# A graph layer's steps: the PSUM copies on VectorE, four more columns a step on ScalarE, another order at the beginning

## The chip, the cores and the metric

The kernel runs on one core of one Trainium2 chip. The metric is the device time of one execution in microseconds (us). A profile of one execution shows TensorE (PE for matmuls, PEld for the loading of weights), VectorE (DVE), ScalarE (ACT), GpSimd (POOL), SyncE (SP) and the DMA queues; a "q" behind an engine's name (ACTq, DVEq, SPq) marks instructions that its sequencer alone works off, such as register loads and DMA issues. PSUM is the memory that TensorE writes to, SBUF the working memory.

## The reference: what is computed

A message-passing layer on a graph of 12,500 nodes (64 features each) and 212,500 edges (32 features each), sorted by destination, with a residual and a layer norm:

```python
msg_in = concat([nodes[row], nodes[col], edge_features])      # 64 + 64 + 32
messages = relu(msg_in @ mW1 + mb1) @ mW2 + mb2               # hidden 128, out 64
aggregated = segment_sum(messages, col, num_segments=12500)
upd_in = concat([nodes, aggregated])
new = relu(upd_in @ uW1 + ub1) @ uW2 + ub2
out = layernorm(x + new)
```

`row` is the source and `col` the destination of an edge.

## The kernel before

**Groups and steps.** The edges are cut into G = 554 groups of 384 (three tiles of 128). One pass of the loop at line 854 is one step k. TensorE's work in step k (`step`, line 806) belongs to three groups: `turn` (460) transposes the gathered source features and a one-hot of the destination of group k into PSUM (line 466, three transposes); `hidden` (487) multiplies the columns of group k-3 with the weights (492); `sums` (517) adds the ReLU results of group k-6 by destination with the one-hot (521). Two PSUM slots alternate (`SLOTS`), so that TensorE's step k waits until what step k-2 left in its slot has been read: by the copy of line 479 and by the ReLU of line 503. After TensorE's step k one instruction copies the transposes together with the sums (513 columns) from PSUM to the operand ring in SBUF (line 479, on ScalarE), and VectorE applies the ReLU for group k-3 (line 503). The last ten groups (`SHORT`) run in another, shorter order.

**Three ways to a group's source features.** Most come by GpSimd's indirect DMA, one for each tile of 128 edges (line 194), issued `AHEAD` = 16 groups ahead into a ring of `RING` = 20. For some groups, the `COPIED` ones, they aren't gathered: the whole transposed node table lies in SBUF (`own.xc`), and ScalarE and VectorE copy single columns of it into the operand ring. The column's address is loaded into a register first (`registers`, 689, the loads are at line 702), then `fetch` (709) issues the copies: VectorE two columns with one instruction (line 725), ScalarE one column with each (line 728). In a step VectorE makes columns in portions of `VCOLS` = (12, 8, 8), ScalarE in portions of `ACOLS` = (8, 4, 4, 4, 4); each portion is one load of that many registers and then its copies. That is 52 columns a step from step 18 on (`BEGIN`), which makes 71 groups `COPIED`. They are complete one step before the group's `turn` step, three before the `hidden` step that reads them. For eight tiles SP fetches single rows (line 783).

**VectorE's order in a step** is ReLU, load of 12 registers, 6 pairs, the one-hot of a later group (line 440), load of 8, 4 pairs, load of 8, 4 pairs. **ScalarE's** is copy, load of 8, 8 columns, then four times load of 4, 4 columns. Every 8 steps VectorE turns the next node numbers into addresses (lines 681 and 687).

**Beginning.** In the first 25 steps `projected(k)` (402) makes the destination half of the first product for 512 nodes: TensorE (407), a ScalarE copy to one of three scratch buffers `t` (410) and a DMA to the table `by_dst` (411). In the first 16 steps `bit(k)` (252) loads a further part of the node table and of the source numbers. `window(g)` (414) loads 32 rows of `by_dst` for group g (line 430); it is issued in step g-4, behind everything that has been stored to `by_dst` so far (`written`). All these DMAs go through SP's queue in program order. At step 8 (`CHECKED`) the sortedness of the edges is checked.

**Updates.** When a chunk of nodes has all its sums (`PLAN`, line 75; 512 nodes, the last full chunk in two halves of 256), `update` (538) works it off in twelve stages, one for each step: its partial sums are loaded (560) and joined on TensorE (571), VectorE moves them out of PSUM (598), three products follow on TensorE (576, 615, 616), a ReLU on ScalarE (621), the last products (627, 628) and the layer norm. All use the one PSUM buffer `u_ps`.

Of the kernel before, what the change touches and what calls it, by code (L numbers as in the profile page):

```python
# [10 lines left out]
F32 = mybir.dt.float32  # L11
# [3 lines left out]
AF = mybir.ActivationFunctionType  # L15
# [5 lines left out]
P = 128  # L21
N = 12500
# [10 lines left out]
G = (E + GE - 1) // GE  # L33
SB = 4
AHEAD = 16
RING = AHEAD + 4
BLOCKS = 4
NW = 8
SLOTS = 2
# [5 lines left out]
AT = BANK - GE  # L45
# [3 lines left out]
CH = 512  # L49
NEAR_NODES = 1024  # L50
NEAR_GROUPS = 16
BITS = 16
LIMITS = (0, 12, 18)
SHORT = 10
# [4 lines left out]
VCOLS = (12, 8, 8)  # L59
ACOLS = (8, 4, 4, 4, 4)  # L60
PAIRED = sum(VCOLS)
# [13 lines left out]
def plan():  # L75


    import math

    def least(g):  # L80
        q = min(1.0, g * GE / E)
        return g * GE * N / E - 6.0 * math.sqrt((E - N) * q * (1 - q)) * N / E - 6

    chunks, b = [], 0
    whole = N // CH * CH
    for e in [*range(CH, whole, CH), whole - CH // 2, whole, N]:
        chunks.append((b, e - b, next((g for g in range(G) if least(g) >= e), G)))
        b = e
    return chunks
# [46 lines left out]
def ordered(ctx: ExitStack, tc: tile.TileContext, a, own, ok):  # L136
# [3 lines left out]
    nc = tc.nc  # L140
    x, out = a["x"], a["out"]
    const = ctx.enter_context(tc.tile_pool(name="const", bufs=1))
    dram = ctx.enter_context(tc.tile_pool(name="dram", bufs=1, space=DRAM))
    rowp = ctx.enter_context(tc.tile_pool(name="rows", bufs=3))
    iop = ctx.enter_context(tc.tile_pool(name="iota_ps", bufs=1, space=PSUM))
# [3 lines left out]
    temp = early.enter_context(tc.tile_pool(name="temp", bufs=1))  # L149
    ident, wm = own.ident, own.wm  # L150
    xc = own.xc[:, 1 : 2 * NP + 1].rearrange("p (n s) -> p n s", s=2)[:, :, 0]
    xc_bytes = own.xc.bitcast(U8)
# [11 lines left out]
    efs_by, hidden_by, marks_by = {}, {}, {}  # L164
# [111 lines left out]
    halves = [(0, G // 2), (G // 2, G)]  # L276
    firsts_f = [own.pre[k][:, : g1 - g0] for k, (g0, g1) in enumerate(halves)]
    for f, (g0, g1) in zip(firsts_f, halves):
# [15 lines left out]

    high = temp.tile([1, G], F32, name="high")
    nc.vector.memset(high, float(N - 1))
    for g0, g1 in zip(LIMITS, [*LIMITS[1:], FIRST_FREE]):
        nc.vector.memset(high[:, g0:g1], float(CH * (1 + max(1, g0 - 6)) - W))
    start_f = temp.tile([1, G], F32, name="start_f")
    start_b = const.tile([1, G, 2], I32, name="start_b")  # L300
# [37 lines left out]
    store_by = {}  # L338
    written = []

# [10 lines left out]
    def ordered_edges():  # L351
# [4 lines left out]
        nc.vector.tensor_scalar(off, dlc, W - 1.0, 0.0, ALU.is_le, ALU.add, accum_out=valid[:, 1:2])  # L356
        low = temp.tile([1, G], F32, name="low")
        opens = [0, *(closes for *_, closes in PLAN)]
# [4 lines left out]
        nc.vector.memset(high[:, 0:1], 0.0)  # L363
        wrong = temp.tile([1, 2, G], F32, name="wrong")
        nwrong = temp.tile([1, 2], F32, name="nwrong")
        first_f = start_f
        nc.vector.tensor_copy(first_f, first_i[0:1, :])
        nc.vector.tensor_tensor(wrong[:, 0], first_f, low, ALU.is_lt)
# [33 lines left out]
    def projected(c):  # L402

        base, n = TABLE[c]
        ps = ups.tile([H, CH], F32, name="u_ps").rearrange("p (n h) -> p n h", n=4)
        for j in range(n):
            nc.tensor.matmul(ps[:, j], xc[: D + 1, base + j * P :][:, :P], w1b,  # L407
                             start=True, stop=True)
        t = rowp.tile([P, 4, H], F32, name="t")
        nc.scalar.activation(t[:, :n], ps[:, :n], AF.Copy)  # L410
        written.append(after(nc.sync.dma_start(
            by_dst[base : base + n * P, :].rearrange("(n p) h -> p n h", n=n), t[:, :n])))

    def window(g):
# [3 lines left out]
        if g % SB == 0:  # L418
# [6 lines left out]
            for i in range(n):  # L425
# [7 lines left out]
                "(w b) -> w b", w=W))  # L433
        after(wm_by[g], *written, *([hidden_by[g - NW]] if g >= NW else []))
        written.clear()

# [23 lines left out]
    def turn(g, ps):  # L460
# [11 lines left out]
        def copy(step):  # L472
            t, c, n = columns(g)
            turn_by[g] = step
            r = slice(D if g in columned else 0, D + W)
            if step in with_sums:
                n = GE + ROW
            copies = [ordered_by_steps(
                after(nc.scalar.activation(t[r, c : c + n], ps[r, AT : AT + n], AF.Copy), step))]  # L479
            if g >= BLOCKS * SB:  # L480
                after(copies[0], hidden_by[g - BLOCKS * SB])
            copy_by[g] = copies
            return copies
# [319 lines left out]
    ahead_of = {turn: 0, hidden: TO_HIDDEN, sums: TO_SUMS}  # L803
    with_sums, unstored = set(), []

    def step(*work):
# [17 lines left out]
        for part, g, _, _, follow in parts:  # L824
            users[part][(g + ahead_of[part]) % SLOTS] = follow(did[-1])
        unstored.extend(g for part, g in work if part is sums)
# [14 lines left out]
    for g in range(SB):  # L841
        window(g)
    nc.sync.dma_start(dlc_i[:, near:], a["dst_cols"][:, near:])
    update_weights()
    weights(NW)
    inputs(1)
    relative(NEAR_GROUPS, G)
    indexes(0)
# [5 lines left out]
    for k in range(G):  # L854
        if k < BITS:
            bit(k)
        if 1 < k < len(TABLE):
            projected(k)
        if k == CHECKED:
            addresses(0)  # L860
            for n in range(len(STREAMS)):
# [24 lines left out]
        if k < G - 1:  # L886
            registers(k, len(VCOLS))
        fetch(0)
        window(k + SB)
        stored()  # L890
# [370 lines left out]
```

## Time and profile before

| | us |
|---|---|
| median of 3 runs | 1848.74 (1846.92 to 1851.61) |
| the profiled execution | 1847.94 |
| its span in the profile | 1846.2 |
| ACT / DVE / POOL / PE busy in the span | 1602.8 / 1151.3 / 1362.1 / 1402.9 |
| mean granted TensorE clock | 0.939 |

The span is the time from the first to the last instruction that the profile shows; the execution is 1.7 us longer. A row of a group of instructions gives line, engine, operation, output<-input and shapes, the count, then busy time, the mean duration of one in ns, and the idle time of the engine just before them with what ended it. "issue" means that nothing which the profile shows was waited for. Loads of registers are not counted as busy time of an engine; the view of one line lists them with their shortest, median and longest duration. In the timeline a row starts with start and length in us.

### The profile page before, as it was taken

Reading aid. Unit: us, or ns where it says so; the run is one execution under the profiler, and the core shown is the slowest. Engines: PE = TensorE matmul, PEld = TensorE weight load, DVE = VectorE, ACT = ScalarE, POOL = GpSimd, SP = SyncE. Lnnn points to the kernel's source line nnn. Section 1 sums busy time; section 2 is a strip of 40 time slices with the busy share of each in tenths; the row PEclk is TensorE's granted clock in tenths of the full one; section 3 lists DMA queues with packets and bytes.
Section 4 is the critical chain, followed back from the end, with each engine's and each line's share of the span. In section 5 each row is a group of like instructions: output and inputs, shape, how many; then the busy total and the mean of one; then the engine's idle time right before and its main releaser. Section 6 shows DMA issues by size and latency. Waiting matters only on the chain. (4 is left out here: it accounts for less than half of the span.)

```text
span 1846.2 us, 57017 instructions
## 1 busy us (share of the span) xinstructions
PE 1402.9 (76%) x9841; PEld 1112.0 (60%) x9841; DVE 1151.3 (62%) x9034; ACT 1602.8 (87%) x13268; POOL 1362.1 (74%) x1447
## 2 busy tenths in 40 slices
PE   3677677877878878768778778777778778788677
PEld 3565565666656656556566566656656556566565
DVE  2315566666666666666666666666666666666652
ACT  2338799999999999899999999989999989989962
POOL 7777577777777777777777777777777777777772
PEclk9759899999999999999999999999989999999999
DMA  6653333333333333333333333333323333333331
GB/s 148 137 132 90 69 74 65 69 76 65 69 75 66 73 72 64 72 61 74 74 65 70 75 64 69 74 64 68 78 63 67 76 63 69 76 63 70 75 65 39
DMA packets 197393, 137.63 MB, mean 75 GB/s; under 512 B 62855, under 2 KB 172653, under 8 KB 196957
## 3 DMA queue, kind: packets, MB, share of 16 engines
q1 hardware_dynamic: 150166, 85.91, 18.7%
q0 software_dynamic: 46080, 47.25, 15.5%
q14 instruction: 288, 2.35, 0.4%
q8 instruction: 85, 1.39, 0.3%
q10 hardware_dynamic: 774, 0.72, 0.2%
HBM read 105.70 MB, written 28.00 MB: 72 GB/s over the span
## 5 line engine op out<-in xcount | busy, mean ns | idle before, releaser
L194 POOL DMA_INDIRECT own_rows<-in_x,src_sb x1440 | 1361.3, 945 | 451.0 <-issue 191.1
L728 ACT ACTIVATE own_operands<-own_xc 64x1 f32 x12576 | 1288.7, 189 | 16.5 <-issue 5.0
L725 DVE TENSOR_TENSOR own_operands<-own_xc 64x2 f32 x7344 | 666.9, 149 | 499.7 <-issue 496.3
L466 PE MATMUL own_ps<-own_ident,own_rows 128*96 128x128 f32 x1653 | 297.8, 292 | 329.9 <-ACT own_operands L728 208.6
L521 PE MATMUL own_ps<-own_h,own_rows 128*32 128x129 f32 x3322 | 491.3, 285 | 4.1 <-ACT own_operands L479 1.9
L492 PE MATMUL own_pre<-own_wm,own_operands 128*128 128x128 f32 x3322 | 490.2, 287 | 0.0
L466 PEld LDWEIGHTS own_ps<-own_ident,own_rows 128*96 128x96 f32 x1653 | 173.0, 133 | 460.4 <-ACT own_operands L728 273.1
L492 PEld LDWEIGHTS own_pre<-own_wm,own_operands 128*128 128x128 f32 x3322 | 443.8, 203 | 2.3 <-issue 1.4
L479 ACT ACTIVATE own_operands<-own_ps 96x513 f32<-96x513 f32 (+2 forms) x554 | 321.1, 580 | 96.0 <-PE own_ps L521 68.5
L503 DVE TENSOR_SCALAR own_h<-own_pre 128x384 f32<-128x384 f32 x553 | 300.4, 543 | 148.2 <-PE own_ps L521 106.9
L521 PEld LDWEIGHTS own_ps<-own_h,own_rows 128*32 128x32 f32 x3322 | 330.5, 113 | 82.7 <-issue 8.6
L440 DVE TENSOR_TENSOR own_rows<-iota,dlc 128x96 f32<-128x96 f32 x554 | 133.7, 242 | 0.1
L571 PE MATMUL u_ps<-own_ident,found 128*1 128x128 f32 (+1 forms) x768 | 100.2, 281 | 19.4 <-DMA found<-by_node 19.0
L571 PEld LDWEIGHTS u_ps<-own_ident,found 128*1 128x1 f32 (+1 forms) x768 | 74.4, 138 | 36.6 <-issue 14.7
L407 PE MATMUL u_ps<-w1b,own_xc 65*128 65x128 f32 x196 | 41.6, 375 | 51.1 <-DMA own_xc<-in_xT_spaced 22.6
L410 ACT ACTIVATE t<-u_ps 128x512 f32<-128x512 f32 (+1 forms) x25 | 14.7, 587 | 70.9 <-DMA by_dst<-t 38.9
L407 PEld LDWEIGHTS u_ps<-w1b,own_xc 65*128 65x128 f32 x196 | 35.4, 268 | 58.3 <-issue 30.5
L576 PE MATMUL u_ps<-own_xc,ux 65*128 65x512 f32 (+1 forms) x50 | 28.5, 650 | 24.1 <-DVE agg L598 24.1
L627 PE MATMUL u_ps<-same,own_xc 65*128 65x64 f32 x192 | 39.6, 288 | 0.5 <-ACT u L621 0.5
L616 PE MATMUL u_ps<-agg,wc 128*128 128x512 f32 (+1 forms) x50 | 39.8, 890 | 0.0
L628 PE MATMUL u_ps<-u,u 128*128 128x64 f32 x192 | 37.1, 275 | 0.0
L627 PEld LDWEIGHTS u_ps<-same,own_xc 65*128 65x128 f32 x192 | 30.3, 197 | 5.7 <-issue 4.2
(92 smaller groups left out, 312.8 us busy)
## 6 DMA issues: line engine op xcount, KB each, us to landing
own_operands<-in_efT SPq DMA_DIRECT2D x138, 192.0 KB
own_rows<-in_x,src_sb POOLq DMA_INDIRECT x1440
by_node<-own_operands SPq DMA_DIRECT2D x554, 32.2 KB
own_side<-in_x SPq DMA_DIRECT2D x1024, 0.2 KB
found<-by_node SPq DMA_DIRECT2D x46, 258.0 KB
own_wm<-by_dst SPq DMA_DIRECT2D x554, 16.0 KB
by_dst<-t SPq DMA_DIRECT2D x24, 256.0 KB
own_xc<-in_xT_spaced SPq DMA_DIRECT2D x12, 358.5 KB
```

Of the source, the lines that this page charges most:

```text
L194: nc.gpsimd.indirect_dma_start(out=s[:p, j, :D], out_offset=None, in_=x[:, :], in_offset=bass.IndirectOffsetOnAxis(ap=src_sb[:p, g * TG + ...
L407: nc.tensor.matmul(ps[:, j], xc[: D + 1, base + j * P :][:, :P], w1b, start=True, stop=True)
L440: places_by[g] = nc.vector.tensor_tensor(own.s[g % RING][:, :, D:], iota.unsqueeze(1).to_broadcast([P, TG, W]), dlc[:, g * TG : (g + 1) * ...
L466: nc.tensor.transpose(xt[:, j * P : j * P + p], sides[g] if g in sides and j == TG - 1 else s[:p, j, :], ident[:p, :p])
L479: after(nc.scalar.activation(t[r, c : c + n], ps[r, AT : AT + n], AF.Copy), step))]
L492: nc.tensor.matmul(pre[:p, j, :], t[:, c + j * P : c + j * P + p], wm[g % NW], start=True, stop=True)
L503: relu_by[g] = [nc.vector.tensor_scalar(h, pre, 0.0, None, ALU.max)]
L521: nc.tensor.matmul(ps[D : D + W, BANK : BANK + ROW], s[:p, j, D:], h[:p, j, :], start=j == 0, stop=j == len(sizes) - 1)
L571: nc.tensor.matmul(ps[:, k * P : (k + 1) * P], t[:, k, w], ident, start=j == 0, stop=j == 1)
L627: nc.tensor.matmul(y[:p, k], xc[: D + 1, nodes[k]], same, start=True, stop=False)
L725: by[engine] = nc.vector.tensor_tensor(o, one, other, ALU.add)
L728: by[engine] = nc.scalar.activation(o, x_at, AF.Copy)
```

## The change

1. **The copy of line 479** goes to VectorE for the groups 16 to 543 (`tensor_copy`); for the others it stays on ScalarE. So that VectorE can issue the columns' first portion in between, the ReLU of a full step is issued only after that portion: `step` puts it on a list, and the loop works the list off after `fetch(0)`.
2. **ScalarE's columns**: one portion of 4 more, 28 a step, 56 with VectorE's 28. `COPIED` follows from that.
3. **The beginning**: a window waits for the chunks of `by_dst` up to number max(1, g-6) only, with four scratch buffers for three; the load of the far destination columns moves from ahead of the loop into step 1, and what VectorE does with them to step 8.
4. **Memory and the end**: gathers go 15 groups ahead (ring of 19); some single-partition tiles move into unused rows of `own.xc`; the destinations of the groups' first edges are converted to floats in place, in SBUF, instead of into PSUM; the last full chunk is cut into 128 and 384 nodes.

```diff
-AHEAD = 16
+AHEAD = 15
-ACOLS = (8, 4, 4, 4, 4)
+ACOLS = (8, 4, 4, 4, 4, 4)
...
-    for e in [*range(CH, whole, CH), whole - CH // 2, whole, N]:
+    for e in [*range(CH, whole, CH), whole - CH * 3 // 4, whole, N]:
...
-    rowp = ctx.enter_context(tc.tile_pool(name="rows", bufs=3))
+    rowp = ctx.enter_context(tc.tile_pool(name="rows", bufs=4))
...
-    firsts_f = [own.pre[k][:, : g1 - g0] for k, (g0, g1) in enumerate(halves)]
+    all_firsts = first_i.bitcast(F32)
+    firsts_f = [all_firsts[:, g0:g1] for g0, g1 in halves]
...
-        written.append(after(nc.sync.dma_start(
-            by_dst[base : base + n * P, :].rearrange("(n p) h -> p n h", n=n), t[:, :n])))
+        written[c] = after(nc.sync.dma_start(
+            by_dst[base : base + n * P, :].rearrange("(n p) h -> p n h", n=n), t[:, :n]))
...
-        after(wm_by[g], *written, *([hidden_by[g - NW]] if g >= NW else []))
-        written.clear()
+        needed = [written.pop(c) for c in sorted(written) if c <= max(1, g - 6)]
+        after(wm_by[g], *needed, *([hidden_by[g - NW]] if g >= NW else []))
...
-            copies = [ordered_by_steps(
-                after(nc.scalar.activation(t[r, c : c + n], ps[r, AT : AT + n], AF.Copy), step))]
+            out_t, in_ps = t[r, c : c + n], ps[r, AT : AT + n]
+            copies = [ordered_by_steps(after(
+                nc.vector.tensor_copy(out_t, in_ps) if NEAR_GROUPS <= g < G - SHORT
+                else nc.scalar.activation(out_t, in_ps, AF.Copy), step))]
...
         for part, g, _, _, follow in parts:
-            users[part][(g + ahead_of[part]) % SLOTS] = follow(did[-1])
+            def followed(part=part, g=g, follow=follow):
+                users[part][(g + ahead_of[part]) % SLOTS] = follow(did[-1])
+
+            if part is hidden and len(parts) == 3:
+                later.append(followed)
+            else:
+                followed()
...
-    nc.sync.dma_start(dlc_i[:, near:], a["dst_cols"][:, near:])
     update_weights()
...
-    relative(NEAR_GROUPS, G)
...
+        if k == 1:
+            nc.sync.dma_start(dlc_i[:, near:], a["dst_cols"][:, near:])
         if k == CHECKED:
+            relative(NEAR_GROUPS, G)
...
         fetch(0)
+        while later:
+            later.pop()()
         window(k + SB)
```

More of the change, by code (lines that the diff above doesn't have):

```diff
@@ L150, in ordered @@
     ident, wm = own.ident, own.wm
+    spare = own.xc[96:97, :]
     xc = own.xc[:, 1 : 2 * NP + 1].rearrange("p (n s) -> p n s", s=2)[:, :, 0]
@@ L293, in ordered @@
     relative(0, NEAR_GROUPS)
-    high = temp.tile([1, G], F32, name="high")
+    high = spare[:, 0 * G : 1 * G]
     nc.vector.memset(high, float(N - 1))
@@ L298, in ordered @@
         nc.vector.memset(high[:, g0:g1], float(CH * (1 + max(1, g0 - 6)) - W))
-    start_f = temp.tile([1, G], F32, name="start_f")
+    start_f = spare[:, 1 * G : 2 * G]
     start_b = const.tile([1, G, 2], I32, name="start_b")
@@ L338, in ordered @@
     store_by = {}
-    written = []
+    written = {}
     up = found_p = None
@@ L356, in ordered_edges @@
         nc.vector.tensor_scalar(off, dlc, W - 1.0, 0.0, ALU.is_le, ALU.add, accum_out=valid[:, 1:2])
-        low = temp.tile([1, G], F32, name="low")
+        low = spare[:, 2 * G : 3 * G]
         opens = [0, *(closes for *_, closes in PLAN)]
@@ L363, in ordered_edges @@
         nc.vector.memset(high[:, 0:1], 0.0)
-        wrong = temp.tile([1, 2, G], F32, name="wrong")
+        wrong = spare[:, 3 * G : 5 * G].rearrange("o (k g) -> o k g", k=2)
         nwrong = temp.tile([1, 2], F32, name="nwrong")
         first_f = start_f
-        nc.vector.tensor_copy(first_f, first_i[0:1, :])
+        nc.vector.tensor_copy(first_f, all_firsts[0:1, :])
         nc.vector.tensor_tensor(wrong[:, 0], first_f, low, ALU.is_lt)
@@ L803, in ordered @@
     ahead_of = {turn: 0, hidden: TO_HIDDEN, sums: TO_SUMS}
-    with_sums, unstored = set(), []
+    with_sums, unstored, later = set(), [], []
     def step(*work):
```

## The prediction

> **What bounds the kernel now.** I read the page first: busy shares, then its groups.
>
> ```profile
> span 1846.2 us, 57017 instructions
> PE 1402.9 (76%) x9841; PEld 1112.0 (60%) x9841; DVE 1151.3 (62%) x9034; ACT 1602.8 (87%) x13268; POOL 1362.1 (74%) x1447
> L194 POOL DMA_INDIRECT own_rows<-in_x,src_sb x1440 | 1361.3, 945 | 451.0 <-issue 191.1
> L728 ACT ACTIVATE own_operands<-own_xc 64x1 f32 x12576 | 1288.7, 189 | 16.5 <-issue 5.0
> L725 DVE TENSOR_TENSOR own_operands<-own_xc 64x2 f32 x7344 | 666.9, 149 | 499.7 <-issue 496.3
> L503 DVE TENSOR_SCALAR own_h<-own_pre 128x384 f32<-128x384 f32 x553 | 300.4, 543 | 148.2 <-PE own_ps L521 106.9
> ```
>
> Two things are to be seen. ACT is the busiest engine, and DVE, at 62%, has 496 us of idle time in front of its column copies that no other engine ends ("issue"). So I asked what the engines do between two columns. Each column's address comes through a register, loaded at L702. These loads are not counted as busy, but the view of that one line shows them. Here it is for ACT over three undisturbed steps and for DVE over one step, then the same three steps of ACT in the timeline:
>
> ```profile
> L702 ACTq TENSOR_LOAD <-index x15: 308/309/548, 1028.7 to 1036.7; - x15
> L702 DVEq TENSOR_LOAD <-index x3: 596/597/845, 1033.7 to 1035.7; - x3
> ```
>
> ```profile
> 1028.96 0.58 ACT L479 ACTIVATE own_operands<-own_ps 96x513 f32<-96x513 f32 x1
> 1029.44 2.44 ACT L728 ACTIVATE own_operands<-own_xc 64x1 f32 x24
> 1031.79 0.58 ACT L479 ACTIVATE own_operands<-own_ps 96x513 f32<-96x513 f32 x1
> ...
> 1034.61 0.58 ACT L479 ACTIVATE own_operands<-own_ps 96x513 f32<-96x513 f32 x1
> 1035.09 2.43 ACT L728 ACTIVATE own_operands<-own_xc 64x1 f32 x24
> 1037.42 0.58 ACT L479 ACTIVATE own_operands<-own_ps 96x513 f32<-96x513 f32 x1
> ```
>
> Three steps take 1037.42 - 1028.96 = 8.46 us, 2.82 each. In each, ACT's sequencer makes five loads: one of 8 registers (0.548) and four of 4 (0.309), together 1.784 us. That leaves 2.82 - 1.784 = 1.036 us to issue 24 columns and one copy, 0.0414 each. Is 2.82 the engine's pace or the sequencer's? Where ACT has been held up before and its instructions stand ready, the same step is shorter:
>
> ```profile
> 978.39 0.57 ACT L479 ACTIVATE own_operands<-own_ps 96x513 f32<-96x513 f32 x1
> 978.87 2.32 ACT L728 ACTIVATE own_operands<-own_xc 64x1 f32 x24
> 981.10 0.57 ACT L479 ACTIVATE own_operands<-own_ps 96x513 f32<-96x513 f32 x1
> ```
>
> 2.71 us: the copy's successor starts 0.48 after it, and the 24 columns go at (2.71 - 0.48) / 24 = 0.093 each. So the engine needs 2.71 and the sequencer 2.82; **ACT is held by its own issue**, and the 0.48 of the copy is the time in which the sequencer gets ahead with the next registers. The columns overlap (189 ns long, 93 apart), which is why a starved ACT still looks busy.
>
> POOL is the other candidate:
>
> ```profile
> L194 POOL DMA_INDIRECT own_rows<-in_x,src_sb x1440: 898/944/1312, 2.9 to 1813.0; - x180
> 500.00:700.00 200.00, 155.19 (x1137) 124.23 (x1136) 135.97 (x1096) 192.89 (x1647) 151.21 (x161) 0.97 0.33 70
> L479 ACT ACTIVATE own_operands<-own_ps x26: 487/587/597, 18.2 to 159.7; 96x513 f32<-96x513 f32 x20, 96x384 f32<-96x384 f32 x6
> L479 ACT ACTIVATE own_operands<-own_ps x517: 572/577/597, 159.7 to 1780.7; 96x513 f32<-96x513 f32 x152, 32x513 f32<-32x513 f32 x21
> ```
>
> The first row is line 194 over the whole run, the second a window of 200 us (the columns are PE, PEld, DVE, ACT, POOL, clock, DMA), the others the step copies up to step 25 and from there on. POOL issues 161 gathers in 200 us, one every 1.242 us; 1440 of them fill 1789 us of the span. The steps take (1780.7 - 159.7) / 516 = 3.141 us each. The two are close; neither has much to give.
>
> **The change part by part.** *Columns on ACT, 24 to 28.* Columns are made from step 18 on; at 56 a step, 76 groups get them instead of 71, so 15 gathers go (1661 tiles - 3 x 76 - 8 = 1425), and they are done at step 539. ACT's copy goes; its sequencer now makes 0.548 + 5 x 0.309 = 2.093 us of loads and issues 28 instructions: 28 x 0.0414 = 1.159. Sum **3.25 us a step**, against 2.82. The other end of the bound is the engine's pace, 28 x 0.093 = 2.60. I take 3.25: nothing is left on ACT that lasts longer than its issue, so the sequencer never gets ahead.
>
> *The copy on DVE.* The nearest row for its length is the PSUM copy of 512 columns; DVE's own step stands below it.
>
> ```profile
> L598 DVE COPY agg<-u_ps 128x512 f32<-128x512 f32 x20 | 13.5, 676 | 0.0
> 1033.79 0.55 DVE L503 TENSOR_SCALAR own_h<-own_pre 128x384 f32<-128x384 f32 x1
> 1034.61 0.51 DVE L725 TENSOR_TENSOR own_operands<-own_xc 64x2 f32 x6 [0.27 <-issue]
> 1035.04 0.24 DVE L440 TENSOR_TENSOR own_rows<-iota,dlc 128x96 f32<-128x96 f32 x1
> 1035.52 0.41 DVE L725 TENSOR_TENSOR own_operands<-own_xc 64x2 f32 x4 [0.24 <-issue]
> 1036.34 0.37 DVE L725 TENSOR_TENSOR own_operands<-own_xc 64x2 f32 x4 [0.40 <-issue]
> 1036.63 0.55 DVE L503 TENSOR_SCALAR own_h<-own_pre 128x384 f32<-128x384 f32 x1
> ```
>
> DVE's step is 1036.63 - 1033.79 = 2.84 us: loads of 0.845 + 0.596 + 0.597 = 2.04, and 0.80 for 16 issues (14 pairs, ReLU, one-hot), 0.05 each. The copy adds 0.68 us of engine time but one issue, 0.05, since the 12-register load runs beside it; the ReLU, moved behind the first six pairs, and the one-hot cover the next 8-register load. Engine time: 0.68 + 0.55 + 0.24 + 14 pairs at (0.51 - 0.15) / 5 = 0.07, about 2.5 us, under 2.89. So the copy costs DVE 0.05 (all hidden) to 0.68 (nothing hidden) a step; I take 0.05. With the 3.14 - 2.84 = 0.30 that its steps now lose, that is 3.19, still below ACT. The copy's wait for TensorE's step holds DVE's pairs behind it, as the ReLU's wait did before; TensorE waits for both two steps later. SP's store of the sums now waits for DVE.
>
> *What else ACT loses a step.* Now 3.14 - 2.82 = 0.32, or 165 us over 516 steps. This is part of it (lines of ACT from 160 to 1782 us):
>
> ```profile
> L479 ACT ACTIVATE own_operands<-own_ps 96x513 f32<-96x513 f32 x447 | 259.7, 581 | 43.7 <-PE own_ps L521 42.0
> L479 ACT ACTIVATE own_operands<-own_ps 32x513 f32<-32x513 f32 x70 | 41.4, 591 | 7.7 <-PE own_ps L521 6.1
> L621 ACT ACTIVATE u<-u_ps 128x512 f32<-128x512 f32 x23 | 13.7, 594 | 18.8 <-PE u_ps L616 18.6
> ```
>
> The copy's waits for TensorE come when a node update holds TensorE up; without copies ACT no longer meets them, and a wait stops the register loads behind it too, so more goes than its idle time. A slower ACT also lets TensorE run ahead, which shortens the wait of L621. I keep 0.11 of the 0.32 (bounds 0 and 0.32): 3.25 + 0.11 = **3.36**.
>
> *The beginning.* Up to step 25 SP's order sets the pace:
>
> ```profile
> 109.54 0.52 SPq L411 DMA_DIRECT2D by_dst<-t  x1
> 114.41 0.60 ACT L410 ACTIVATE t<-u_ps 128x512 f32<-128x512 f32 x1 [6.12 <-DMA by_dst<-t]
> 114.43 0.34 SPq L430 DMA_DIRECT2D own_wm<-by_dst  x1
> 114.90 0.59 ACT L479 ACTIVATE own_operands<-own_ps 96x513 f32<-96x513 f32 x1
> 110.00:130.00 20.00, 15.33 (x66) 12.75 (x65) 2.68 (x12) 3.97 (x14) 15.09 (x16) 0.50 0.62 145
> ```
>
> The store of a projected chunk is issued at 109.54, the next window load behind it at 114.43: 4.9 us of a step of about 7 are its landing. With windows that wait only for chunks up to two steps older, and a fourth buffer, this goes. Late next are DMA (0.62 of 7 us, 4.3) and TensorE at a granted 0.50 (15.33 us in 20, or 5.4 of 7). So 1.6 to 2.7 us for each of some ten steps, something for the rest, and the far half of the destination columns out of the first loads: I take 24 us (bounds 0 and 40), so the copy of step 25 at 159.7 - 24 = **136 us**. ACT can't work ahead of that point, since the projections' copies keep it with TensorE up to step 24.
>
> *At nothing:* one gather group less ahead (with ACT as the bound POOL waits anyway; it costs if POOL is the bound again), the scratch rows moved into spare rows, and the last chunks, 128 and 384 nodes for 256 and 256 (within 3 us either way).
>
> *Sum.* Steps 25 to 539 are 515: 136 + 515 x 3.36 = 1868. The end: TensorE then waits in step 543 for the last columns; the copy of step 541 was at 1780.7, and TensorE began step 543 here:
>
> ```profile
> 1783.02 0.50 PE L466 MATMUL own_ps<-own_ident,own_rows 128*96 128x128 f32 x3 [0.94 <-issue]
> ```
>
> That is 63 us before the end of the span, 1846.2. 1868 + 63 = 1931 of span; the execution took 1.7 more than its span (1847.94 for 1846.2): **1933 us**. That execution lies 0.8 under the median of the three runs, which I leave out.
>
> **The rivals.** *Gathers set the end (faster).* If ACT's columns went at the engine's pace, 2.60 + 0.32 = 2.92 a step, and DVE at 3.19, POOL would be last: 15 x 1.242 = 18.6 us less, 1848 - 18.6 = 1829. It decides from an ACT step under 3.20: (1846 - 136 - 63) / 515. For it: ACT's 2.71 us steps, where loads hide behind waiting columns. Against: the three 2.82 us steps, where they do not, although a copy helps. [...]
>
> *ACT's losses stay.* All 0.32 remains: 3.57 a step, 136 + 1839 + 63 + 1.7 = 2040. For it: the update's chain through TensorE is unchanged. Against: ACT meets it in three instructions of some 22 steps only.
>
> *DVE pays the copy whole.* 2.84 + 0.68 + 0.30 = 3.82: 2168. For it: nothing covers DVE's issue gaps of 0.24 to 0.45 now. Against: the 12-register load already begins before the ReLU ends its 0.55.
>
> **How the numbers follow.** The forecast case 0.81 (its range 1885 to 1995); losses stay 0.08; DVE 0.05; gathers 0.05; and 0.01 that a beginning quicker by another 85 us cancels it. A measurement tells 0.3%, some 5.5 us, from no change; the loss forecast is 85. Faster 0.05, same 0.01, slower 0.94. The range for 8 in 10, 1885 to 1995, holds an ACT step of 3.27 to 3.48 with step 25 at 136, and step 25 from 120 to 155 with ACT steps of 3.30 to 3.44.
>
> **What would show it.** Right: ACT's loads six a step, columns in one stretch of 28 with starts about 0.12 apart and small gaps ended by "issue", steps of 3.3 to 3.4; POOL waiting for ACT or DVE instead of 161 gathers in 200 us; DVE's copy followed by its pairs with a gap under 0.25. Wrong: POOL still at 161 in 200 us (gathers), TensorE's steps started by DVE (rival three), or ACT idle before L621 as long as now or longer (rival two). A step-25 copy outside 120 to 160 us would break the term of the beginning alone.

## The result, and the profile after

| | before | after |
|---|---|---|
| median (4 runs each) | 1850.17 us (1846.92 to 1855.73) | 1980.55 us (1978.70 to 1989.02) |
| span of the profiled execution | 1846.2 us | 1977.5 us |
| mean granted TensorE clock | 0.939 | 0.937 |

The changed kernel takes 1.0724 times as long, with a 95% interval of 1.0691 to 1.0758: **7.2% slower**. The forecast was 1933 us, with a range of 1885 to 1995. The sign and what holds the kernel came as forecast; some 48 us of the size did not. Two later sets of runs, the first with e5, e6, e7 and e8, the second with e7b, e8b and e9, showed the kernel before itself at 2559 and 2531 us, with instructions that start late (in e5 ScalarE's columns, VectorE's step copies and the gathers last 189, 684 and 945 ns, for 189, 680 and 946 in the changed kernel, but 682.8, 422.1 and 1142.7 us of idle time stand in front of them, for 161.7, 91.1 and 552.7), for a cause that stays open, so that from these two only durations and comparisons inside the set are used.

The page of the changed kernel, its span, the busy shares and the groups that answer to those shown of before:

```profile
span 1977.5 us, 59100 instructions
PE 1411.5 (71%) x9841; PEld 1129.1 (57%) x9841; DVE 1442.8 (73%) x9516; ACT 1668.6 (84%) x14752; POOL 1349.2 (68%) x1432
L732 ACT ACTIVATE own_operands<-own_xc 64x1 f32 x14588 | 1594.4, 189 | 161.7 <-issue 130.7
L195 POOL DMA_INDIRECT own_rows<-in_x,src_sb x1425 | 1348.4, 946 | 552.7 <-issue 327.1
L729 DVE TENSOR_TENSOR own_operands<-own_xc 64x2 f32 x7298 | 658.7, 148 | 254.0 <-issue 196.7
L482 DVE COPY own_operands<-own_ps 96x513 f32<-96x513 f32 (+1 forms) x528 | 358.8, 680 | 91.1 <-PE own_ps L525 87.5
L468 PE MATMUL own_ps<-own_ident,own_rows 128*96 128x128 f32 x1653 | 302.6, 294 | 370.4 <-DVE own_h L507 306.9
L575 PE MATMUL u_ps<-own_ident,found 128*1 128x128 f32 (+1 forms) x768 | 136.9, 345 | 124.4 <-ACT count L592 104.6
```

ACT's own share has fallen, from 87% to 84%, and yet ACT is what holds the kernel. A first sign is the idle time in front of the columns: before it was 16.5 us in all, 5.0 of it "issue"; now it is 161.7 us, 130.7 of it "issue". By itself this doesn't tell: the kernel of e2 below, which is as fast as the one before, has 120.9 us of it. What tells is that ACT hardly waits for other engines (8 us from 160 to 1912 us), and that TensorE waits for ACT. At each node update ScalarE copies the nodes' counts out of PSUM (line 592), behind the columns that it is late with, and the update's next product (line 575) waits for that copy: 104.6 us in 22 waits, where the same line of e2 waits 18.7 us in all and for ACT not at all. POOL's 1425 gathers now leave 552.7 us idle for 451.0. DVE makes 528 PSUM copies of 0.68 us, 359 us of work that it didn't have, and its idle time in front of its columns falls from 499.7 to 254.0 us: by this sum most of the copies went into its issue gaps.

The window of 200 us in the middle of the run, as quoted of before (PE, PEld, DVE, ACT, POOL, clock, DMA), and ACT's register loads over 1400 us:

```profile
500.00:700.00 200.00, 145.35 (x1017) 115.66 (x1018) 154.83 (x1036) 181.89 (x1651) 140.19 (x149) 0.94 0.29 63
L706 ACTq TENSOR_LOAD <-index x2466: 304/311/804, 300.1 to 1699.3; - x190
```

149 gathers for 161, one in 1.34 us for 1.24: POOL no longer runs at its own pace. The loads of four registers still take 0.31 us each; there are six loads a step for five.

ACT's timeline over about three steps:

```profile
1001.64 3.34 ACT L732 ACTIVATE own_operands<-own_xc 64x1 f32 x28
1005.23 2.08 ACT L732 ACTIVATE own_operands<-own_xc 64x1 f32 x20 [0.24 <-issue]
1007.60 0.97 ACT L732 ACTIVATE own_operands<-own_xc 64x1 f32 x8 [0.29 <-issue]
1008.83 3.06 ACT L732 ACTIVATE own_operands<-own_xc 64x1 f32 x28 [0.25 <-issue]
1012.15 1.99 ACT L732 ACTIVATE own_operands<-own_xc 64x1 f32 x19 [0.26 <-issue]
```

The stretch ends during the load of 8 registers, and "issue" gaps of about 0.25 us part the steps. One step takes 1012.15 - 1008.83 = 3.32 us. The two ahead of it take 3.59 and 3.60: the first has 28 columns in 3.34 us instead of 3.06, the second is broken by a further gap of 0.29 after 20 columns. So a quiet step of ACT has 3.32 us, and some have one more gap of 0.28.

The other engines don't go at this pace. VectorE's copies in a quiet stretch and at an update of the changed kernel, and at the same update of e6b (below), where ACT is quicker:

```profile
L482 DVE COPY own_operands<-own_ps x5: 675/676/679, 631.9 to 643.4; 96x513 f32<-96x513 f32 x5
L482 DVE COPY own_operands<-own_ps x2: 679/684/690, 664.8 to 674.0; 96x513 f32<-96x513 f32 x2
```

```profile
L482 DVE COPY own_operands<-own_ps x2: 675/676/677, 635.5 to 638.9; 96x513 f32<-96x513 f32 x2
```

Between updates they come (643.4 - 631.9) / 4 = 2.87 us apart, and ACT falls behind. At the update one step takes 9.2 us, for 3.4 in e6b, until ACT has caught up. So ACT's 3.41 us a step on the average are paid in one long step at each update.

### The profile page after: what moved, and what is told of

Same layout as the page of the kernel before. It is cut to its first block, busy times and chain, and to the rows that moved or that the text cites. A ratio compares the mean times of both kernels' runs of the same rounds, so it can differ in the third digit from the quotient of the medians.

```text
span 1977.5 us, 59100 instructions
## 1 busy us (share of the span) xinstructions
PE 1411.5 (71%) x9841; PEld 1129.1 (57%) x9841; DVE 1442.8 (73%) x9516; ACT 1668.6 (84%) x14752; POOL 1349.2 (68%) x1432
## 3 DMA queue, kind: packets, MB, share of 16 engines
q14 instruction: 306, 2.51, 0.4%
## 5 line engine op out<-in xcount | busy, mean ns | idle before, releaser
L732 ACT ACTIVATE own_operands<-own_xc 64x1 f32 x14588 | 1594.4, 189 | 161.7 <-issue 130.7
L195 POOL DMA_INDIRECT own_rows<-in_x,src_sb x1425 | 1348.4, 946 | 552.7 <-issue 327.1
L729 DVE TENSOR_TENSOR own_operands<-own_xc 64x2 f32 x7298 | 658.7, 148 | 254.0 <-issue 196.7
L468 PE MATMUL own_ps<-own_ident,own_rows 128*96 128x128 f32 x1653 | 302.6, 294 | 370.4 <-DVE own_h L507 306.9
L525 PE MATMUL own_ps<-own_h,own_rows 128*32 128x129 f32 x3322 | 482.2, 282 | 4.0 <-ACT own_operands L483 1.7
L496 PE MATMUL own_pre<-own_wm,own_operands 128*128 128x128 f32 x3322 | 481.8, 284 | 0.0
L496 PEld LDWEIGHTS own_pre<-own_wm,own_operands 128*128 128x128 f32 x3322 | 435.6, 200 | 1.9 <-issue 1.4
L482 DVE COPY own_operands<-own_ps 96x513 f32<-96x513 f32 (+1 forms) x528 | 358.8, 680 | 91.1 <-PE own_ps L525 87.5
L575 PE MATMUL u_ps<-own_ident,found 128*1 128x128 f32 (+1 forms) x768 | 136.9, 345 | 124.4 <-ACT count L592 104.6
L575 PEld LDWEIGHTS u_ps<-own_ident,found 128*1 128x1 f32 (+1 forms) x768 | 107.3, 198 | 145.4 <-ACT count L592 110.5
L602 DVE COPY agg<-u_ps 128x512 f32<-128x512 f32 (+2 forms) x25 | 16.7, 669 | 76.6 <-PE u_ps L575 76.6
L483 ACT ACTIVATE own_operands<-own_ps 96x384 f32<-96x384 f32 (+2 forms) x26 | 13.5, 520 | 44.5 <-PE own_ps L468 20.8
```

The lines of the kernel that those rows point to most:

```text
L195: nc.gpsimd.indirect_dma_start(out=s[:p, j, :D], out_offset=None, in_=x[:, :], in_offset=bass.IndirectOffsetOnAxis(ap=src_sb[:p, g * TG + ...
L468: nc.tensor.transpose(xt[:, j * P : j * P + p], sides[g] if g in sides and j == TG - 1 else s[:p, j, :], ident[:p, :p])
L482: nc.vector.tensor_copy(out_t, in_ps) if NEAR_GROUPS <= g < G - SHORT
L496: nc.tensor.matmul(pre[:p, j, :], t[:, c + j * P : c + j * P + p], wm[g % NW], start=True, stop=True)
L525: nc.tensor.matmul(ps[D : D + W, BANK : BANK + ROW], s[:p, j, D:], h[:p, j, :], start=j == 0, stop=j == len(sizes) - 1)
L575: nc.tensor.matmul(ps[:, k * P : (k + 1) * P], t[:, k, w], ident, start=j == 0, stop=j == 1)
```

## The experiments

The theories:

- **A**: ScalarE's register loads and the issue of its columns add up to its step, and nothing else holds the changed kernel.
- **B**: the way of the copy and the sums through VectorE holds TensorE, and the 28 columns only happen to be there.

Each edit is to the changed kernel, if nothing else is said.

### e1: the copy back on ScalarE, 28 columns kept

```diff
-                nc.vector.tensor_copy(out_t, in_ps) if NEAR_GROUPS <= g < G - SHORT
-                else nc.scalar.activation(out_t, in_ps, AF.Copy), step))]
+                nc.scalar.activation(out_t, in_ps, AF.Copy), step))]
...
-            if part is hidden and len(parts) == 3:
+            if False:
```

> The changed kernel with the copy back on ScalarE and the ReLU back in its old place; 28 columns on ScalarE, the new beginning and last chunks stay. Theory A (ScalarE's own issue of loads and columns sets the step): one more issue a step, 0.04 us, and the waits for TensorE come back, up to 0.2 us: ScalarE step 3.45 to 3.6, total 2000 to 2080 us. Theory B (the copy on VectorE and the waits through it set the step): without it the time falls to 1850 to 1900 us.

Measured: 2020.95 us (2014.79 to 2024.58), 1.0921 times before (1.0885 to 1.0957). The largest wait of TensorE from 300 to 1700 us, ACT's copies from 160 to 1950 us, and two steps of ACT's timeline (a copy is left out):

```profile
PEld own_ps L468 <- ACT own_operands L482: 449.8, 310, 2.3
```

```profile
L482 ACT ACTIVATE own_operands<-own_ps 96x513 f32<-96x513 f32 x438 | 253.8, 579 | 3.7 <-PE own_ps L524 2.0
```

```profile
1001.30 2.87 ACT L731 ACTIVATE own_operands<-own_xc 64x1 f32 x28
1004.19 0.59 ACT L482 ACTIVATE own_operands<-own_ps 96x513 f32<-96x513 f32 x1
1004.69 2.83 ACT L731 ACTIVATE own_operands<-own_xc 64x1 f32 x28
...
1007.91 3.12 ACT L731 ACTIVATE own_operands<-own_xc 64x1 f32 x28
```

The kernel without the copy on VectorE is slower still, by 40 us, so the move itself is no loss and B falls. A step here is 3.39 and 3.22 us: 0.58 us of copy beside 28 columns makes it hardly longer than the 3.32 without one. That fits the trace of before, where the sequencer loads the next registers while the copy runs: the copy that lasts from 1028.96 to 1029.54 has this load beside it.

```profile
L702 ACTq TENSOR_LOAD <-index x1: 548/548/548, 1028.7 to 1028.7; - x1
```

The 40 us are 40 / 515 = 0.08 us a step, half of it the copy's one issue by the prediction's 0.0414; the other half isn't divided. And ACT's copies wait 3.7 us for TensorE here, where those of before waited 43.7: with the slower ACT these waits are nearly gone, here with the copies on ScalarE, and in the changed kernel without them (0.8 us behind TensorE's line 525, in the row of ACT's columns below). TensorE now waits for ACT, 449.8 us in the row above.

### e2: the copy on VectorE, 24 columns

```diff
-ACOLS = (8, 4, 4, 4, 4, 4)
+ACOLS = (8, 4, 4, 4, 4)
```

> The changed kernel with 24 columns a step on ScalarE (five loads) instead of 28; the copy stays on VectorE. Theory A: ScalarE's issue falls to 0.548 + 4 x 0.309 + 24 x 0.0414 = 2.78 us, no longer the bound; 1440 gathers (one in 1.242 to 1.249 us) or VectorE at about 3.1 to 3.2 us a step set the end: 1820 to 1870 us. Theory B: the step stays near 3.4, 1930 us or more.

Measured: 1849.72 us (1843.76 to 1852.67), 0.999 times before (0.9973 to 1.0007). The middle of its run and two starts of ACT's stretches:

```profile
500.00:700.00 200.00, 152.96 (x1108) 121.35 (x1108) 169.08 (x1151) 169.32 (x1559) 151.22 (x161) 0.97 0.32 70
1004.70 2.55 ACT L732 ACTIVATE own_operands<-own_xc 64x1 f32 x24 [0.33 <-issue]
1007.49 2.55 ACT L732 ACTIVATE own_operands<-own_xc 64x1 f32 x24 [0.24 <-issue]
```

The whole loss is in the four columns: 1980.55 - 1849.72 = 131 us. ACT's step is 2.79 us, so four columns and one load cost 3.32 - 2.79 = 0.53 us of ACT, near the 0.309 + 4 x 0.0414 = 0.47 of the prediction's rows. And POOL is back at 161 gathers in 200 us, its own pace, as before. The copy's move with the rest of the change, but without the four columns, is worth nothing here.

### e3: 28 columns, two loads of 14

```diff
-ACOLS = (8, 4, 4, 4, 4, 4)
+ACOLS = (14, 14)
```

> The changed kernel with ScalarE's 28 columns in two portions of 14 (two register loads a step) instead of 8 and five times 4 (six loads). A load of 4 takes 0.309 us and one of 8 0.547, so 0.06 a register and 0.07 a load: two loads of 14 take about 1.81 us instead of 2.09, 0.28 less a step. Theory A: ScalarE step near 3.1 us, total 1830 to 1870 us, where gathers or VectorE take over. Theory B: no change, 1970 to 1990 us.

Measured: 2959.02 us, 1.6 times before (1.5959 to 1.6042). A miss of over 1000 us. The register loads, and ACT's timeline:

```profile
L706 ACTq TENSOR_LOAD <-index x378: 1212/2122/3404, 1000.2 to 1999.7; - x189
1501.35 1.41 ACT L732 ACTIVATE own_operands<-own_xc 64x1 f32 x14 [2.10 <-issue]
1503.05 1.41 ACT L732 ACTIVATE own_operands<-own_xc 64x1 f32 x14 [0.29 <-issue]
1506.57 1.41 ACT L732 ACTIVATE own_operands<-own_xc 64x1 f32 x14 [2.11 <-issue]
```

I had taken a load's time to fall with the number of loads. In the trace the loads of 14 alternate between about 1.2 us (1.212 the shortest) and 3.0 (an estimate: the median, 2.122, lies midway between two kinds of equal number), and the engine stands for 2.1 us in front of every second portion. If a step's first portion starts on a register number that four divides, the second, 14 further, doesn't. Both lengths then fit one rule. By the loads of the prediction, 0.309 us for 4 and 0.548 for 8, a four costs 0.24 and a load 0.07 besides. With 0.215 us for each register outside of an aligned four, twelve in fours and two alone are 0.07 + 3 x 0.24 + 2 x 0.215 = 1.22, and fourteen alone 0.07 + 14 x 0.215 = 3.08. That is an estimate from the two lengths; e6 tests the part with the fours. The second load also begins 42 numbers into the step's 56 in memory, which four doesn't divide either, so whether the register's number or the place in memory makes the difference isn't shown. For theory A the kernel still speaks: with loads of 4.2 us a step instead of 2.1 the step grows from 3.41 to 1506.57 - 1501.35 = 5.22 us, and the copy's way through VectorE is the same.

### e4 and e5: the window's wait at the beginning

```diff
-    by_dst = dram.tile([NP, H], F32, name="by_dst")
+    by_dst = nc.dram_tensor("own_by_dst", (NP, H), F32, kind="Internal").ap()
```

> The changed kernel with the table of projected rows held in a plain DRAM tensor, so that a window's load waits only for the chunks that the changed lines name and not for the newest store. If that wait is why the beginning came out long, SP's 4 us waits ahead of line 430 go and the copy of step 25 falls from 154 to about 136 us: total 1955 to 1970 us. If DMA or TensorE at half clock hold the beginning, step 25 stays at 148 us or later and the total within 6 us of 1980.

e5 named every later store as one that the window doesn't depend on, from group 12 on, and issued the store of the sums ahead of the window load:

```diff
+        for later_store in written.values() if g >= 12 else ():
+            tc.declare_no_dep(wm_by[g].ins, later_store.ins.name, reason="a window's rows lie in earlier chunks")
...
-        window(k + SB)
...
+        window(k + SB)
```

> The changed kernel, with the window's loads freed by name from the stores of newer chunks (from group 12 on), and issued behind the store of the sums instead of ahead of it. In the plain DRAM tensor the wait for the newest store was still there (SP stood 4.3 us ahead of line 432), so that run told nothing of its cost. If that wait holds the beginning: step 25 at 130 to 145 us instead of 154, total 1955 to 1972. If DMA or TensorE's clock holds it: step 25 at 148 or later, total 1974 to 1988.

Measured: e4 1981.59 us (1978.60 to 1988.26), 1.0709 times before, as the changed kernel; e5 2573.62 us, 1.0061 times before in its set (1.0044 to 1.0078). SP's queue in the beginning of the changed kernel, and what SP's window loads waited for between 60 and 160 us there, in e4 and in e5 (us in total, times, longest):

```profile
109.37 0.52 SPq L413 DMA_DIRECT2D by_dst<-t  x1
113.99 0.34 SPq L432 DMA_DIRECT2D own_wm<-by_dst  x1
SPq L432 <- DMA by_dst<-t: 46.2, 16, 4.4
```

```profile
SPq L432 <- DMA own_by_dst<-t: 43.6, 15, 4.3
```

```profile
SPq L432 <- DMA by_dst<-t: 7.5, 3, 3.0
135.13 0.41 SPq L413 DMA_DIRECT2D by_dst<-t  x1
...
136.93 0.47 SPq L432 DMA_DIRECT2D own_wm<-by_dst  x1
```

In the changed kernel and in e4 the window load stands until the store ahead of it has landed, here 4.6 us after its issue. The kernel before has 47.0 us of these waits, also 16, so the diff, which names older chunks alone, took none away; what puts the wait there isn't known, and e4 is without a result. e5 did take it away: the three waits that are left are those of groups 9 to 11, ahead of the edit, and from group 12 on the window load follows a store by as little as 1.8 us. So e5 can say what the wait was worth. The ten step copies on VectorE up to step 25 in e5, and in e6 of the same set, which has the changed kernel's beginning:

```profile
L484 DVE COPY own_operands<-own_ps x10: 677/690/692, 161.8 to 204.6; 96x513 f32<-96x513 f32 x9, 32x513 f32<-32x513 f32 x1
```

```profile
L482 DVE COPY own_operands<-own_ps x10: 677/690/692, 162.0 to 204.5; 96x513 f32<-96x513 f32 x9, 32x513 f32<-32x513 f32 x1
```

Step 25 comes at 204.6 us without the wait and at 204.5 with it (202.5 and 203.1 in e7 and e8). SP's wait for the landing is gone, and the beginning is no shorter: in this set of runs something else held it. The expectation names DMA and TensorE's clock, the late starts themselves are a third, and which it was isn't shown. Outside such a set the edit wasn't run.

### e6: 28 columns, loads of 12 and 16

```diff
-ACOLS = (8, 4, 4, 4, 4, 4)
+ACOLS = (12, 16)
```

> The changed kernel with ScalarE's 28 columns in portions of 12 and 16. Loads of 4, 8 and 12 registers took 0.309, 0.547 and 0.83 us; the loads of 14 took 1.22 and 3.04 us, as if whole fours that begin on a four cost 0.24 to 0.28 and every other register 0.21. By that, 12 and 16 take 0.83 + 1.07 = 1.9 us against 2.09 for six loads: 0.19 less a step. Theory A (ScalarE's issue): ScalarE step 3.40 - 0.19 = 3.21, total 1980 - 98 = 1882 (1850 to 1900). If the hand-over through VectorE were the bound: 1970 to 1990. If long loads are slow for their length: above 1990.

> The changed kernel with ScalarE's 28 columns loaded in two groups, 12 and 16, instead of 8 and five fours. Theory A (ScalarE's register loads and its issue of columns add up to its step): the loads take 0.80 + 1.00 = 1.80 us instead of 2.09, the step falls from 3.31 to about 3.03 us in quiet steps, and the time to 1981 - 515 x 0.28 = about 1840 us, if the gathers don't end it later (1829 us at the least by the prediction): 1825 to 1890 us. Theory B (the way of the copy and the sums through VectorE sets the step): 1960 to 1985 us, as the changed kernel.

Measured as e6, in the first set of the late starts: 2477.65 us, 0.9687 times before (0.9666 to 0.9708), and 96 us less than e5, which has the loads of the changed kernel. The same kernel as e6b: **1838.07 us** (1836.12 to 1842.69) for 1848.18 before (1847.50 to 1854.57), a ratio of 0.9937 (0.9915 to 0.9958). The loads, ACT's timeline from 1010 us on, the middle of e6b's run and the row of its columns:

```profile
L706 ACTq TENSOR_LOAD <-index x898: 767/1002/1074, 299.8 to 1699.0; - x180
1009.89 8.21 ACT L732 ACTIVATE own_operands<-own_xc 64x1 f32 x82
500.00:700.00 200.00, 147.99 (x1105) 117.61 (x1104) 169.26 (x1147) 178.98 (x1805) 151.21 (x161) 0.99 0.32 70
L732 ACT ACTIVATE own_operands<-own_xc 64x1 f32 x14588 | 1429.4, 187 | 158.3 <-issue 73.4
```

This one line of source separates the theories: the copy's way and the 28 columns stay, the loads fall to at most 0.77 + 1.00 = 1.77 us a step by the shortest and the median of the row (two loads of alternating size), and the time falls by 1980.55 - 1838.07 = 142 us. TensorE's row at line 575 has 19.7 us of idle time left, none of it ended by ACT's count. **A holds**, with one correction. ACT here runs 82 columns in a row without a gap that the view opens, 8.21 / 82 = 0.10 us each, or 2.80 a step, where 3.03 was expected and 1.77 + 28 x 0.0414 would be 2.93: the prediction's 0.0414 is not a fixed price of a column, and comes to (2.80 - 1.77) / 28 = 0.037 with two loads. Such stretches are not the whole: 158.3 us of idle time stand in front of the columns, 73.4 of them "issue", and now ACT waits for other engines too. The gathers go at their own pace again, 161 in 200 us, and from 300 to 1700 us POOL never waits longer than 0.3 us. But TensorE's steps start on VectorE's ReLU in the same stretch (276 waits of the weight loads), so whether the gathers or VectorE's step would end a faster kernel isn't separated. Twelve registers take 0.77 us, where e3's rule gives 0.07 + 3 x 0.24 = 0.79, and sixteen 1.00, where it gives 1.03.

It is the only kernel here, outside the late starts, that is below the kernel before, by 0.6%, a small difference that the interval keeps clear of none. Fifteen gathers less would be 18.6 us at 1.242; what is left of them can be read in POOL's row (the prediction shows that of before, with the last gather at 1813.0):

```profile
L195 POOL DMA_INDIRECT own_rows<-in_x,src_sb x1425: 898/946/1403, 2.9 to 1802.4; - x179
```

The last gather comes 10.6 us earlier, the end 5.2 us (1841.0 of span for 1846.2; the profiled execution of e6b, 1842.69 us, is the longest of its four). So 8 us of the 18.6 go while gathers still run, and 5.4 behind the last one.

### e7: one load of 28; VectorE's columns in 12 and 16

```diff
-VCOLS = (12, 8, 8)
-ACOLS = (8, 4, 4, 4, 4, 4)
+VCOLS = (12, 16)
+ACOLS = (28,)
```

> The changed kernel with ScalarE's 28 columns in one portion and VectorE's in 12 and 16. ScalarE's load by the same rule 1.75 to 1.85 us: its issue 3.0 us a step; VectorE's loads 1.9 instead of 2.04. Theory A: neither is the bound any more, the 1425 gathers are (one in 1.248 us, 1778 us): 1830 to 1850 us, faster than before. If one long portion starves ScalarE's engine more than it saves: 1870 to 1950.

> The changed kernel with ScalarE's 28 columns loaded in one group of 28 and VectorE's 28 in 12 and 16 (before: 8 and five fours; 12, 8 and 8). Loads of 1.73 us on ScalarE and 0.84 + 1.09 = 1.93 us on VectorE (2.04 before). Theory A: ScalarE's step by its issue would be 1.73 + 1.16 = 2.9 us; with 161 gathers in 200 us already reached at 12 and 16, the gathers set the end, and the time stays at that of 12 and 16, 1838 us, within 10 us (1828 to 1848). If VectorE's step were the bound at 12 and 16, its 0.11 us less would give up to 50 us less (1790 to 1825), which the gathers exclude by theory A. Theory B (the way of the copy through VectorE): 1960 us or more.

Measured: 2547.98 us, 0.9951 times before (0.9934 to 0.9968), and as e7b 2525.20 us, 0.9978 (0.9954 to 1.0001), in the first and the second set of the late starts. That leaves the times without an answer to what was asked, but not the durations. ACT's loads, the load between two quiet steps, and these steps, in e7b:

```profile
L706 ACTq TENSOR_LOAD <-index x323: 1702/1727/2089, 301.3 to 1699.5; - x162
L706 ACTq TENSOR_LOAD <-index x1: 1727/1727/1727, 1035.2 to 1035.2; - x1
1033.62 2.71 ACT L732 ACTIVATE own_operands<-own_xc 64x1 f32 x28 [1.02 <-issue]
1037.05 2.71 ACT L732 ACTIVATE own_operands<-own_xc 64x1 f32 x28 [0.72 <-issue]
```

The load is 1.73 us, as expected, and the step is not: 1037.05 - 1033.62 = 3.43 us, where loads and issue add up to 1.73 + 1.16 = 2.89. The 28 columns run at the engine's pace, 2.71 us, and then ACT is idle for 0.72. So the 28 are not issued in 1.16 us here: the sequencer has 3.43 - 1.73 = 1.70 for them. The last column starts 27 x 0.093 = 2.51 us after the first, at 1036.13, and the next load begins at 1035.2, 0.9 us ahead of it: the sequencer is then 0.9 / 0.093, about ten columns, ahead of the engine. Ten columns last 10 x 0.093 = 0.93 us: the load of 1.73 us is 0.80 longer, near the 0.72 for which ACT is idle, and one of 1.00 us, as e6b has, would be 0.07 longer (estimates from this one load). That fits e6b, whose step of 2.80 is 0.2 above 28 x 0.093, but it rests on quiet steps of a run with late starts, and one load of 28 wasn't run outside of them.

### e8 and e9: 60 columns; the loads of 12 in the kernel before

e8 is the changed kernel with 60 columns, e9 the kernel before with 52 and ScalarE's registers in two loads:

```diff
-VCOLS = (12, 8, 8)
-ACOLS = (8, 4, 4, 4, 4, 4)
+VCOLS = (12, 20)
+ACOLS = (28,)
```

```diff
-VCOLS = (12, 8, 8)
-ACOLS = (8, 4, 4, 4, 4)
+VCOLS = (12, 16)
+ACOLS = (12, 12)
```

> As the run with 28 in one portion, with VectorE at 12 and 20 columns: 60 a step, 82 groups by columns, 1407 gathers (1756 us). VectorE: loads 0.85 + 1.3, 19 issues at 0.05: 3.1 us a step, with what else it loses 3.2 to 3.4. If gathers set the end: 1810 to 1830 us. If VectorE does: 1840 to 1900.

> The changed kernel with 60 columns a step: 28 on ScalarE in one load, 32 on VectorE in loads of 12 and 20. 1407 gathers instead of 1425. Theory A, gathers as the bound at 56 columns: 18 gathers less at 1.24 us are 22 us less, about 1816 us (1805 to 1830), if VectorE's step, 0.84 + 1.3 of loads and 0.05 x 19 of issue = 3.1 us, doesn't come to bind; if it does, 1830 to 1880 us.

> The kernel before, with its copy on ScalarE and 52 columns, but with ScalarE's 24 registers loaded in 12 and 12 instead of 8 and four fours, and VectorE's in 12 and 16. ScalarE's loads fall from 1.784 to about 1.6 us; by theory A its quiet step falls from 2.82 to about 2.7, the engine's own pace. Its 1440 gathers at 1.242 us fill 1789 us already: with the gathers as the bound it gains 5 us or less (1840 to 1855 us); if ScalarE's losses to the updates were the bound, 515 x 0.1 = 50 us less (1795 to 1820 us).

Measured, all in the two sets of the late starts: e8 2542.13 us, 0.9925 times before (0.9896 to 0.9953); e8b 2505.19 us, 0.9900 (0.9877 to 0.9923); e9 2456.68 us, 0.9707 (0.9672 to 0.9741). The engines don't keep their pace there (120 gathers from 500 to 700 us in e7b and 123 in e9, for 161 before), so nothing follows for a set in which the kernel before takes 1850 us. Whether 60 columns or the better loads without the rest of the change would beat e6b's 1838 us stays open.

## Why the prediction came out as it did

**ACT held by its own issue: right.** It is shown by e2 and e6b, each with one tuple changed: 131 us come back with four columns less, 142 us with the same columns and shorter loads. How ACT holds the others was not in the prediction: not step by step, but by TensorE's wait at each update, 104.6 us. One sign that the prediction had named for being wrong did come, TensorE's steps started by DVE (306.9 of the 370.4 us in the row of line 468). It doesn't speak for rival three: e6b has it as well (322.0 us), at 1838 us.

**The step, 3.25 us of loads and issue: 0.07 short.** The quiet step is 3.32. At 24 columns without the copy the same prices give 1.784 + 24 x 0.0414 = 2.78, and e2 measured 2.79; the term that was short is the sixth load with its four columns, 0.53 where the sum has 0.309 + 4 x 0.0414 = 0.47. Why it costs more than the others isn't shown.

**The 0.11 kept of what ACT loses: near in size, and from another source.** ACT's lines between 160 and 1912 us, and its last columns:

```profile
L732 ACT ACTIVATE own_operands<-own_xc 64x1 f32 x14355 | 1568.8, 189 | 153.1 <-issue 128.0 <-PE own_ps L525 0.8 <-DVE own_operands L482 0.5
L625 ACT ACTIVATE u<-u_ps 128x512 f32<-128x512 f32 x23 | 13.2, 573 | 0.0
```

```profile
1909.00 2.99 ACT L732 ACTIVATE own_operands<-own_xc 64x1 f32 x28
```

The wait ahead of the update's ReLU (now L625) is gone, 18.8 us before and 0.0 now, and so are the 51 us ahead of the copies: rival two, 2040 us, falls by the sign that was named for it. The reason given for the copies' part, that ACT no longer makes them, is not needed: in e1 it makes them and waits 5.5 us (3.7 in the row above, 1.8 for the copies of 32 rows). What is left is 6.6 us ahead of one count copy and the further gap of 0.28 us in some steps. The 515 steps from the copy of step 25 (153.8, below) to the end of the last columns, 1909.00 + 2.99 = 1911.99, take (1911.99 - 153.8) / 515 = 3.414 us each. So 0.09 stands beside the quiet 3.32, for the 0.11 kept; in all 3.414 for 3.36, which is 0.054 x 515 = 28 us of the miss.

**The copy on DVE, 0.05 us a step: right.** DVE's timeline behind one copy:

```profile
1001.73 0.68 DVE L482 COPY own_operands<-own_ps 96x513 f32<-96x513 f32 x1
1002.53 0.51 DVE L729 TENSOR_TENSOR own_operands<-own_xc 64x2 f32 x6
1002.96 0.55 DVE L507 TENSOR_SCALAR own_h<-own_pre 128x384 f32<-128x384 f32 x1
```

Six pairs follow the copy 0.12 us after its end (1002.53 - 1002.41): the load of 12, 0.842 us from 1001.6 on, ran beside it. In quiet stretches, where TensorE's steps start on DVE's ReLU, DVE's step is 2.87 us, for 2.84 + 0.05 forecast. Rival three, 2168 us, falls; e6b shows that DVE with the copy keeps up with 3.15 us a step on the average.

**The beginning, 24 us: mis-sized. The step that failed is the one that said of the landing "this goes", and that 1.6 to 2.7 us a step come of it.** The copies on DVE up to 155.3 us, steps 16 to 25:

```profile
L482 DVE COPY own_operands<-own_ps x10: 679/690/692, 106.2 to 153.8; 96x513 f32<-96x513 f32 x9, 32x513 f32<-32x513 f32 x1
```

The copy of step 25 came at 153.8 us, 5.9 earlier than before and 17.8 later than the 136 forecast. The window load still waits for the store just ahead of it (109.37 to 113.99). I had read in the diff which chunks a window names, and taken its waits to be those; the trace shows that another order is kept. And e5, where the wait did go, has its step 25 no earlier than e6 of the same set, so the wait may not be what held the beginning at all. Nothing else of it was tested, and the 5.9 us aren't divided.

**The gathers as the bound, 1829 us: not here, but near where it was put.** The rival was to decide at an ACT step under 3.20 us, at 1829 us. e6b's ACT needs 2.80 us in the stretch above; its steps take 3.15 on the average, from (1775.5 - 155.1) / 515 in this row of its copies, and the time is 1838 us:

```profile
L482 DVE COPY own_operands<-own_ps x516: 655/678/693, 155.1 to 1775.5; 96x513 f32<-96x513 f32 x150, 32x513 f32<-32x513 f32 x22
```

**The end, 63 us:** 1977.5 - 1911.99 = 65.5, 2.5 more. The prediction's own sum is 2 us off: 136 + 515 x 3.36 is 1866, not 1868, and the span 1929. The miss of the span from there is the sum of the three: 17.8 + 27.8 + 2.5 = 48.1, for 1977.5 - 1929.4.

## What to carry to other kernels

Where each copy takes its address from a register, count the register loads and the issue of a step before adding copies, since the profile's busy share shows neither: idle time that ends in "issue", in short pieces at the same place in every step, is a first sign, and what decides is that the engine waits for nobody while others wait for it. Size the loads by what the waiting columns can cover (here 12 and 16 ran 82 columns in 8.21 us without a gap that the view opens, while six small ones and one of 28 left ScalarE idle for 0.25 and 0.72 us in a quiet step), and prefer whole fours to 14 (0.77 us for 12 and 1.00 for 16, but 1.2 and 3.0 in turn for 14). A wait that a diff seems to take away is only gone when the queue's timeline shows it gone, and to take it away brings only as much as the next limit allows.

## What the runs showed of the hardware that was not expected

- A load of registers took 0.31 us for 4, 0.77 for 12, 1.00 for 16 and 1.73 for 28, but 1.2 and 3.0 in turn for 14: about 0.06 us a register in fours, and 0.215 outside of them (estimates; that the alignment makes the difference is argued from e3's two lengths, no run moved an equal load by one register).
- One longer load was not better than two here: 28 in one load take 3.43 us a step (quiet steps of e7b), 12 and 16 take 2.8 (e6b). The sequencer was only about ten columns ahead of ScalarE when the load of 28 began.
- A copy of 0.58 us on ScalarE made its step hardly longer (3.22 and 3.39 us in e1, 3.32 without); in the trace of before a register load of 0.548 us runs beside such a copy.
- ScalarE falls behind in every step of the changed kernel (3.32 us in a quiet one, for 2.87 of VectorE between updates), and that came back at one place: 22 waits of TensorE at the node updates, 104.6 us in all.
- In some steps of the changed kernel one more gap of 0.28 us opens, at no fixed column; its cause was not looked for.
